# Gated cross-attention: score and weight transposes moved from TensorE to VectorE, softmax on half rows

## The chip, the cores and the metric

The kernel runs on one core of a Trainium2 chip. The metric is the device time of one execution in microseconds. Five engines work side by side, each through its own queue in order: TensorE (PE, with its weight loads PEld), VectorE (DVE), ScalarE (ACT), GpSimd (POOL) and SyncE (SP), which issues most of the DMAs.

## The reference

Input x has 8 batches of 1024 tokens of 1024 features; each batch has a memory of 64 rows of 512 features. All is float32.

```python
memory_proj = einsum('bme,de->bmd', memory, W_mem)
scores = einsum('bnd,bmd->bnm', hidden_states, memory_proj) / sqrt(D)
attn = softmax(scores, axis=-1)
memory_context = einsum('bnm,bmd->bnd', attn, memory_proj)
gate_input = concatenate([hidden_states, memory_context], axis=-1)
gate = sigmoid(einsum('bnf,df->bnd', gate_input, W_gate) + b_gate)
fused = hidden_states + gate * memory_context
return fused * rsqrt(mean(fused ** 2) + 1e-6) * norm_w
```

## The kernel before

A setup of some 78 us loads the weights, projects the memory (`mp`, the keys, and `mg`, which is the memory times the second half of the gate weights) and prepares sums of weights. Then 16 tiles of 512 tokens follow, 53.8 us each.

The product of a tile with the first half of the gate weights is done by two nested layers of a seven-product scheme for 2x2 block matrices. The outer layer has seven products, in the order 1, 6, 7, 5, 4, 2, 3 (`ORDER`); each is made of seven inner products of four matmul records, one per **slot**, so that a tile has 49 slots. `outer_product` writes the inner products to the PSUM banks `af`, `ed` (two sets, used in turn), `b` (`kB`) and `c` (`kC`). Banks b and c exist once: the next writer has to wait until DVE has read them in `u2 = p1 + kB` and `u3 = u2 + kC`. ACT copies `p1` out of `af`, DVE adds `u2`, `u3`, `u4`, POOL adds u3 and u4 into the blocks of the result (`pre`), and DVE then adds `ed` and `af` (`fin_ed`, `fin_af`). POOL also prepares the left sides of the next outer product (`inner_s`, tiles `l`).

In the outer products 4 and 3, `visit` multiplies the transposed attention weights `attnT` with the memory (tiles `pc`) and adds their gate part to `af` and `ed`. Its first two result tiles lie in banks b and c.

The attention itself is small. `scores` computes the scores transposed (memory rows on partitions: 64 rows for each of two halves of the tokens) into two banks, ACT and DVE join them in `sT`. `transpose_scores` turns `sT` by two PE transposes into PSUM (`sc`), `softmax_a` takes the maximum of each row on DVE and runs four exponentials with bias and row sum on ACT, `softmax_b` takes the reciprocal and scales by four ACT operations, and `transpose_attn` turns the result by two PE transposes (`pa`), from where four ACT copies fill `attnT`. `attn_difference` makes the differences of weights that the gate part needs.

What sets the order is written out by hand: `plan` puts each step in a slot with `at(t0 + n, ...)`, or beside a product with `mid`, and every engine gets its instructions in just that program order (`keep_in_program_order`).

Of the kernel before, what the change touches and what calls it, by code (L numbers as in the profile page):

```python
# [8 lines left out]
F32 = mybir.dt.float32  # L9
AF = mybir.ActivationFunctionType  # L10
ALU = mybir.AluOpType
AX = mybir.AxisListType
# [3 lines left out]
P = 128  # L16
# [4 lines left out]
def tile_gated_cross_attention_rmsnorm(  # L21
# [42 lines left out]
    nc = tc.nc  # L64
    B, N, D = x.shape
    M, E = mem.shape[1:]
# [8 lines left out]
    NPAIR = BM // P  # L75
    SCALE = 1.0 / float(D) ** 0.5
    Q4 = D // 4

    const = ctx.enter_context(tc.tile_pool(name="const", bufs=1))
    gpool = ctx.enter_context(tc.tile_pool(name="gpool", bufs=7))  # L80
# [3 lines left out]
    small = ctx.enter_context(tc.tile_pool(name="small", bufs=1))  # L84
    ps = ctx.enter_context(tc.tile_pool(name="ps", bufs=1, space=PSUM))
    ps_ctx = ctx.enter_context(tc.tile_pool(name="ps_ctx", bufs=2, space=PSUM))
    dram = ctx.enter_context(tc.tile_pool(name="dram", bufs=1, space=DRAM))

    pin = tc.keep_in_program_order

    def mm(o, lhsT, rhs, start, stop):
        pin(nc.tensor.matmul(o, lhsT, rhs, start=start, stop=stop, skip_group_check=True))  # L92

    def tt(eng, o, a, b, op):
        pin(eng.tensor_tensor(o, a, b, op))  # L95
# [4 lines left out]
    def t4k(pool, shape, tag, name):  # L100
        return pool.tile(shape, F32, tag=tag, name=name)
# [31 lines left out]
    for k in range(KD):  # L133
        t = t4k(*((gpool, [P, D], "gate") if k < 7 else (apool, [P, D], "s4")), f"w2_{k}")
# [40 lines left out]
    ident = const.tile([P, P], F32, name="ident")  # L175
# [160 lines left out]


    A, S, L2, O = {}, {}, {}, {}
    sTs, attns, attnTs, scs, dens, mps, mgs = {}, {}, {}, {}, {}, {}, {}
    def where(q, t=0):  # L340
        return q // QPB, (q % QPB) * QT + t * P

# [79 lines left out]
        tt(nc.vector, flat, flat, part, ALU.add)  # L422
        sTs[q] = sT

    def transpose_scores(q):
        sc = ps_ctx.tile([P, 4, M], F32, tag="ctx", name=f"sc{q}")
        sT = sTs.pop(q)
        for t in range(2):
            pin(
                nc.tensor.transpose(  # L430
                    sc[:, 2 * t : 2 * t + 2, :].rearrange("p r m -> p (r m)"), sT[:, t, :], ident
                )
            )
        scs[q] = sc

    def softmax_a(q):
        sc = scs.pop(q)
        mx = t4k(small, [P, 4], "mx", f"mx{q}")
        pin(nc.vector.tensor_reduce(mx, sc, AX.X, ALU.max))
        pin(nc.scalar.activation(mx, mx, AF.Copy, scale=-SCALE))  # L440
        e = attns[q] = t4k(small, [P, 4, M], "e", f"e{q}")
        den = dens[q] = t4k(small, [P, 4], "den", f"den{q}")
        for t in range(4):
            pin(
                nc.scalar.activation(
                    e[:, t], sc[:, t], AF.Exp, bias=mx[:, t : t + 1], scale=SCALE, accum_out=den[:, t : t + 1]
                )
            )

    def softmax_b(q):  # L450
        e, den = attns[q], dens.pop(q)
        pin(nc.vector.reciprocal(den, den))
        for t in range(4):
            pin(nc.scalar.activation(e[:, t], e[:, t], AF.Copy, scale=den[:, t : t + 1]))

    def transpose_attn(q):
        attn = attns.pop(q)
        pa = ps_ctx.tile([P, 2, P], F32, tag="ctx", name=f"pa{q}")
        for t in range(2):
            pin(  # L460
                nc.tensor.transpose(  # L461
                    pa[:, t, :],
                    attn[:, 2 * t : 2 * t + 2, :].rearrange("p r m -> p (r m)"),
                    ident,
                )
            )

        at = attnTs[q] = t4k(small, [P, 8, P], "attnT", f"attnT{q}")
        for g in (1, 0):
            for r in range(2):  # L470
                pin(
                    nc.scalar.copy(
                        at[g * M : (g + 1) * M, 2 * r : 2 * r + 2, :], pa[r * M : (r + 1) * M]
                    )
                )

    def attn_difference(q):
        at = attnTs[q]
        tt(nc.vector, at[M:P, 4:6, :], at[M:P, 0:2, :], at[M:P, 2:4, :], ALU.subtract)
        tt(nc.vector, at[M:P, 6:8, :], at[M:P, 2:6:2, :], at[M:P, 3:6:2, :], ALU.subtract)  # L480

    def load_mp(b):
        mps[b] = t4k(small, [P, KD, M], "mpb", f"mpb{b}")
# [132 lines left out]
    def at(slot, fn, *args):  # L616
        due.setdefault(slot, []).append(lambda: fn(*args))
# [202 lines left out]
    def visit(q, o, pcs, af, ed):  # L820

        row, h, g = EXT[o]
        at_, mg = attnTs[q], mgs[q // QPB]
        second = o in SECOND
        for r, k in ((0, af), (1, ed)):
            cols = slice(h * H, (h + 1) * H)
            for t in TOKENS:
                mm(pcs[r][t, :], at_[0:M, 2 * row + r, t], mg[0:M, cols], True, True)
            if second and r == 0:
                for n, left in ((0, g + r), (1, NEG[o])):  # L830
                    part = mg[M:P, h * H + n * C : h * H + (n + 1) * C]
                    for t in TOKENS:
                        mm(k[t, n], at_[M:P, left, t], part, False, True)
# [193 lines left out]
```

## Time and profile before

| what | value |
| --- | --- |
| median of three runs | 953.74 us (953.54 to 953.8) |
| span of the profiled execution | 951.8 us |
| its own time | not listed apart from its span; the median of the runs is 1.9 us above the span |
| mean granted TensorE clock | 0.997 |
| one tile (414.5 to 468.3 us) | PE busy 53.80, DVE 45.96, ACT 21.79, POOL 39.92 us |
| PE transposes of scores and weights | 32 of `sc`, 32 of `pa` |

The span runs from the first instruction to the last. A row of the timeline gives start and duration in us, engine, line, operation, output and inputs by the program's names, shape and count; brackets hold the idle time of the engine ahead of it and what ended it. Instructions of one engine overlap at their ends, so the step from one start to the next is the price of one on a busy engine.

### The profile page before, as it was taken

What the parts mean: (1) busy time and instruction counts of PE and PEld (TensorE: products, weight loads), DVE (VectorE), ACT (ScalarE), POOL (GpSimd) and SP (SyncE); (2) the same over time, 40 slices, a digit from 0 to 9 for tenths busy, and PEclk for the clock granted to TensorE, in tenths of its full rate; (3) what the DMA queues carried; (4) which work ended last, traced back from release to release, by engine and by line L of the source; (5) the groups of instructions that cost most, each with busy time, mean ns of one, the idle gap of its engine ahead of it and who ended that gap; (6) DMA issues with size and microseconds to landing.
All of it is one profiled execution on the core that took longest, in us unless ns stands there. A gap on an engine that the chain in (4) does not pass through costs nothing.

```text
span 951.8 us, 15584 instructions
## 1 busy us (share of the span) xinstructions
PE 939.9 (99%) x5624; PEld 732.1 (77%) x5624; DVE 806.5 (85%) x1258; ACT 361.9 (38%) x782; POOL 711.0 (75%) x780
## 2 busy tenths in 40 slices
PE   9999999999999999999999999999999999999995
PEld 8546778787877778787877778687877778787773
DVE  6988888888888888888888888888888888888887
ACT  3001235162433525153443526253443526243456
POOL 5997877688676777787686867777686767877683
PEclk9999999999999999999999999999999999999998
DMA  9956664482919365481918366391918466390632
GB/s 377 285 144 161 105 122 112 108 181 48 206 46 185 98 130 131 103 185 39 217 45 174 93 141 138 90 199 32 215 53 166 101 133 144 79 210 25 144 142 89
DMA packets 70923, 128.40 MB, mean 135 GB/s; under 512 B 12352, under 2 KB 49216, under 8 KB 70592
## 3 DMA queue, kind: packets, MB, share of 16 engines
q1 hardware_dynamic: 61664, 93.86, 37.5%
q0 software_dynamic: 9184, 33.56, 19.4%
q8 instruction: 45, 0.74, 0.3%
q14 instruction: 30, 0.25, 0.1%
HBM read 87.56 MB, written 41.68 MB: 136 GB/s over the span
## 4 chain that ended last, share of the span: by engine, by line
PE 97%; DVE 2%; ACT 1%; issue 0%; DVEq 0%
PE af L92 31%; PE ed L92 21%; PE pc L92 10%; PE kC L92 10%; PE kB L92 10%; PE pg L92 5%; PE psT_af L92 5%; PE pm L92 3%; DVE gate L95 1%; PE psT_ed L92 0%; PE pz L92 0%; DVE gate L788 0%; PE sc L430 0%; PE pa L461 0%; PE psT_b L92 0%; PE pt L193 0%
## 5 line engine op out<-in xcount | busy, mean ns | idle before, releaser
L95 POOL TENSOR_TENSOR gate<-gate,u 128x512 f32<-128x512 f32 (+1 forms) x224 | 236.9, 1070 | 187.4 <-DVE u L95 151.3
L685 ACT ACTIVATE gate<-gate 128x512 f32<-128x512 f32 x128 | 80.2, 630 | 225.0 <-DVE gate L95 225.0
L352 DVE STREAM_TRANSPOSE a<-xq 128x512 f32<-128x512 f32 x128 | 141.5, 1108 | 3.4 <-issue 3.4
L95 POOL TENSOR_TENSOR l<-a 128x256 f32<-128x256 f32 x128 | 110.9, 866 | 18.6 <-PE af L92 17.5
L714 DVE SCALAR_TENSOR_TENSOR gate<-gate,ss,nw_sb 128x512 f32<-128x512 f32 x120 | 119.4, 995 | 1.1
L92 PE MATMUL pc<-mg,attnT 64*64 64x512 f32 x512 | 116.8, 595 | 0.1
L92 PE MATMUL ed<-it,l 128*128 128x256 f32 x448 | 115.0, 379 | 0.0
L92 PE MATMUL kB<-it,l 128*128 128x256 f32 x448 | 115.0, 379 | 0.0
L95 DVE TENSOR_TENSOR gate<-gate,pc 128x512 f32<-128x512 f32 x128 | 86.1, 682 | 31.7 <-ACT gate L685 31.7
L901 ACT COPY u<-af 128x256 f32<-128x256 f32 x112 | 40.7, 363 | 182.6 <-PE af L92 182.6
L92 PE MATMUL af<-w,a 128*128 128x256 f32 x384 | 98.5, 379 | 0.0
L92 PEld LDWEIGHTS kB<-it,l 128*128 128x128 f32 x448 | 85.1, 190 | 11.6
L95 DVE TENSOR_TENSOR gate<-gate,ed 128x512 f32<-128x512 f32 x112 | 76.1, 679 | 19.1 <-POOL gate L95 17.5
L92 PEld LDWEIGHTS ed<-it,l 128*128 128x128 f32 x448 | 83.9, 190 | 10.7
L95 DVE TENSOR_TENSOR gate<-gate,af 128x512 f32<-128x512 f32 (+1 forms) x128 | 76.7, 609 | 12.8 <-PE af L92 11.2
L92 PEld LDWEIGHTS af<-w,a 128*128 128x128 f32 x384 | 73.0, 190 | 10.3 <-issue 0.5
L95 POOL TENSOR_TENSOR l<-s 128x256 f32<-128x256 f32 x96 | 78.2, 814 | 3.3 <-DVE it L95 3.3
L92 PEld LDWEIGHTS pc<-mg,attnT 64*64 64x64 f32 x512 | 32.9, 132 | 50.1 <-issue 23.5
L92 PE MATMUL af<-mg,attnT 64*64 64x256 f32 (+1 forms) x384 | 67.4, 456 | 0.0
L92 PE MATMUL ed<-it,a 128*128 128x256 f32 x256 | 67.4, 386 | 0.0
L95 DVE TENSOR_TENSOR u<-u,kC 128x256 f32<-128x256 f32 x112 | 45.9, 410 | 23.8 <-PE kC L92 20.3
L92 PE MATMUL af<-t,s 128*128 128x256 f32 x256 | 65.8, 379 | 0.0
(147 smaller groups left out, 2044.6 us busy)
## 6 DMA issues: line engine op xcount, KB each, us to landing
xq<-in_x SPq DMA_DIRECT2D x64, 512.0 KB, 10.3
gate<-in_x POOLq DMA_DIRECT2D x60, 512.0 KB, 8.4
out<-gate SPq DMA_DIRECT2D x60, 512.0 KB, 3.3
w<-in_w_gate_t SPq DMA_DIRECT2D x8, 512.0 KB, 10.2
w<-in_w_gate_t SPq DMA_DIRECT2D x2, 2048.0 KB, 17.2
mg<-mgd SPq DMA_DIRECT2D x16, 256.0 KB, 5.2
wm<-in_w_mem_t SPq DMA_DIRECT2D x4, 512.0 KB, 6.0
mpd<-mpT SPq DMA_DIRECT2D x4, 512.0 KB, 8.6
```

The costliest lines, as they stand in the source:

```text
L92: pin(nc.tensor.matmul(o, lhsT, rhs, start=start, stop=stop, skip_group_check=True))
L95: pin(eng.tensor_tensor(o, a, b, op))
L352: nc.vector.transpose(A[key][:, :, r * P : (r + 1) * P], chunks(xq[q][:, 4 * t : 4 * t + 4, :], KD)[:, half * KH : (half + 1) * KH],)
L685: pin(nc.scalar.activation(g, g, AF.Sigmoid))
L714: nc.vector.scalar_tensor_tensor(g[:, cols], g[:, cols], rstd[:, t % 2 : t % 2 + 1], nw_sb[:, cols], ALU.mult, ALU.mult,)
L901: pin(nc.scalar.copy(p1, af[:, 0]))
```

## The change

The four PE transposes of a tile go. DVE transposes blocks of 32x32 instead, which leaves a row of 64 memory rows split in two halves of 32 that lie on different groups of 32 partitions. Each half gets its maximum (and its sum) by a DVE reduction; four ACT copies of 32x8 elements bring the other half's value beside it; DVE joins the two. The subtraction of the maximum and the division by the sum are POOL operations over the whole tile, and the exponential is one ACT operation. DVE transposes the weights back into the first two of eight `attnT` blocks; two ACT copies of 64 partitions fill the next two. `visit` and `attn_difference` use the blocks in the new places (`upper`). The steps stand in slots 9, 10, 12, 15, 17, 20 and 23 where they stood in 9, 10, 13, 18 and 22.

```diff
-    def transpose_scores(q):
-        sc = ps_ctx.tile([P, 4, M], F32, tag="ctx", name=f"sc{q}")
...
-                nc.tensor.transpose(
-                    sc[:, 2 * t : 2 * t + 2, :].rearrange("p r m -> p (r m)"), sT[:, t, :], ident
+    def turn_scores(q):
+        sc = scs[q] = t4k(small, [P, 2 * P // B32, B32], "sc", f"sc{q}")
+        pin(nc.vector.transpose(sc.rearrange("p n m -> p (n m)"), sT.rearrange("p t c -> p (t c)")))
+        mx = mxs[q] = t4k(small, [P, 2, 8], "mx", f"mx{q}")
+        pin(nc.vector.tensor_reduce(mx[:, 0], sc, AX.X, ALU.max))
+    def other_half(o, i):
+        for g in range(4):
+            pin(nc.scalar.copy(o[g * B32 : (g + 1) * B32], i[(g ^ 1) * B32 : ((g ^ 1) + 1) * B32]))
+    def spread(v):
+        return v.unsqueeze(2).to_broadcast([P, 8, B32])
+    def softmax_a(q):
+        other_half(mx[:, 1], mx[:, 0])
+    def softmax_b(q):
+        tt(nc.vector, mx[:, 0], mx[:, 0], mx[:, 1], ALU.max)
+        tt(nc.gpsimd, sc, sc, spread(mx[:, 0]), ALU.subtract)
+        pin(nc.scalar.activation(sc, sc, AF.Exp, scale=SCALE))
+    def softmax_c(q):
+        pin(nc.vector.tensor_reduce(den[:, 0], scs[q], AX.X, ALU.add))
+        other_half(den[:, 1], den[:, 0])
+    def softmax_d(q):
+        tt(nc.vector, den[:, 0], den[:, 0], den[:, 1], ALU.add)
+        pin(nc.vector.reciprocal(den[:, 0], den[:, 0]))
+        tt(nc.gpsimd, sc, sc, spread(den[:, 0]), ALU.mult)
+    def turn_attn(q):
+            nc.vector.transpose(
+                at[:, 0:2].rearrange("p t c -> p (t c)"), sc.rearrange("p n m -> p (n m)")
...
-        at(t0 + 9, transpose_scores, q)
+        at(t0 + 9, turn_scores, q)
         at(t0 + 10, softmax_a, q)
-        at(t0 + 13, softmax_b, q)
-        at(t0 + 18, transpose_attn, q)
-        at(t0 + 22, attn_difference, q)
+        at(t0 + 12, softmax_b, q)
+        at(t0 + 15, softmax_c, q)
+        at(t0 + 17, softmax_d, q)
+        at(t0 + 20, turn_attn, q)
+        at(t0 + 23, attn_difference, q)
...
-                    mm(whole[t, :], at_[M:P, g + r, t], mg[M:P, cols], second, True)
+                    mm(whole[t, :], at_[M:P, upper(g + r), t], mg[M:P, cols], second, True)
```

On POOL, before, between the outer products 6 and 5 of the seventh tile (in a name such as `u_7_3085` the 7 is the outer product; `l_6_5` is the left side of outer product 5 in that tile):

```order
L95 TENSOR_TENSOR gate_0_3025<-gate_0_3025,u_6_3030 128x256
L95 TENSOR_TENSOR l_6_5_3090<-s_6_2955 128x256
L95 TENSOR_TENSOR l_6_5_3090<-l_6_5_3090,s_6_2955 128x256
L95 TENSOR_TENSOR l_6_5_3090<-s_6_2955 128x256
L95 TENSOR_TENSOR l_6_5_3090<-s_6_2955,l_6_5_3090 128x256
L95 TENSOR_TENSOR gate_3_3103<-gate_1_3017,u_7_3085 128x512
L95 TENSOR_TENSOR gate_2_3120<-gate_0_3025,u_7_3085 128x256
```

The same place now:

```order
L96 TENSOR_TENSOR gate_0_3019<-gate_0_3019,u_6_3024 128x256
L96 TENSOR_TENSOR sc_3039<-sc_3039,mx_3041 128x256
L96 TENSOR_TENSOR l_6_5_3078<-s_6_2949 128x256
L96 TENSOR_TENSOR l_6_5_3078<-l_6_5_3078,s_6_2949 128x256
L96 TENSOR_TENSOR l_6_5_3078<-s_6_2949 128x256
L96 TENSOR_TENSOR l_6_5_3078<-s_6_2949,l_6_5_3078 128x256
L96 TENSOR_TENSOR gate_3_3097<-gate_1_3011,u_7_3073 128x512
L96 TENSOR_TENSOR sc_3039<-sc_3039,den_3081 128x256
L96 TENSOR_TENSOR gate_2_3109<-gate_0_3019,u_7_3073 128x256
```

The subtraction stands ahead of the four `l` and of the `pre` of outer product 7, the multiplication right behind that `pre`.

On DVE, before, from the end of outer product 7 to the first adds of outer product 4 in the same tile:

```order
L95 TENSOR_TENSOR gate_3_3103<-gate_3_3103,ed_7_3084 128x512
L352 STREAM_TRANSPOSE a_7_3125<-xq_2996 128x4x128
L95 TENSOR_TENSOR gate_2_3120<-gate_0_3025,af_7_3083 128x256
L95 TENSOR_TENSOR gate_2_3120<-gate_2_3120,af_7_3083 128x256
L352 STREAM_TRANSPOSE a_7_3125<-xq_2996 128x4x128
L95 TENSOR_TENSOR attnT_3112<-attnT_3112 64x256 x2
L95 TENSOR_TENSOR u_5_3133<-u_5_3133,kB_5_3146 128x256
L352 STREAM_TRANSPOSE a_7_3155<-xq_2996 128x4x128
L95 TENSOR_TENSOR u_5_3133<-u_5_3133,kC_5_3157 128x256
L352 STREAM_TRANSPOSE a_7_3155<-xq_2996 128x4x128
L95 TENSOR_TENSOR u_5_3133<-u_5_3133,ed_5_3132 128x256
L95 TENSOR_TENSOR u_4_3177<-u_4_3177,kB_4_3184 128x256
```

The same place now, up to the point from which the rows are the same again:

```order
L96 TENSOR_TENSOR gate_3_3097<-gate_3_3097,ed_7_3072 128x512
L468 STREAM_TRANSPOSE attnT_3114<-sc_3039 128x256
L353 STREAM_TRANSPOSE a_7_3118<-xq_2990 128x4x128
L96 TENSOR_TENSOR gate_2_3109<-gate_0_3019,af_7_3071 128x256
L96 TENSOR_TENSOR gate_2_3109<-gate_2_3109,af_7_3071 128x256
L353 STREAM_TRANSPOSE a_7_3118<-xq_2990 128x4x128
L96 TENSOR_TENSOR u_5_3126<-u_5_3126,kB_5_3137 128x256
L96 TENSOR_TENSOR attnT_3114<-attnT_3114 64x256 x2
L353 STREAM_TRANSPOSE a_7_3148<-xq_2990 128x4x128
```

The transpose of the weights is put in ahead of four transposes of the next tile's x, and `attn_difference` has changed places with the kB add of outer product 5. Above this place, the transpose of the scores, the two reductions, the two joins and the reciprocal stand among the adds of outer products 6 and 7.

More of the change, by code (lines that the diff above doesn't have):

```diff
@@ L77, in tile_gated_cross_attention_rmsnorm @@
     Q4 = D // 4
+    B32 = 32
     const = ctx.enter_context(tc.tile_pool(name="const", bufs=1))
@@ L423, in add_scores @@
         sTs[q] = sT
-    def transpose_scores(q):
-        sc = ps_ctx.tile([P, 4, M], F32, tag="ctx", name=f"sc{q}")
+    def turn_scores(q):
         sT = sTs.pop(q)
-        for t in range(2):
-            pin(
-                nc.tensor.transpose(
-                    sc[:, 2 * t : 2 * t + 2, :].rearrange("p r m -> p (r m)"), sT[:, t, :], ident
-                )
-            )
[L434 to L475, printed above, removed]
+        sc = scs[q] = t4k(small, [P, 2 * P // B32, B32], "sc", f"sc{q}")
@@ new lines, in softmax_b @@
+    def softmax_b(q):
+        sc, mx = scs[q], mxs.pop(q)
+        tt(nc.vector, mx[:, 0], mx[:, 0], mx[:, 1], ALU.max)
+        tt(nc.gpsimd, sc, sc, spread(mx[:, 0]), ALU.subtract)
+        pin(nc.scalar.activation(sc, sc, AF.Exp, scale=SCALE))
+    def softmax_c(q):
+        den = dens[q] = t4k(small, [P, 2, 8], "den", f"den{q}")
+        pin(nc.vector.tensor_reduce(den[:, 0], scs[q], AX.X, ALU.add))
+        other_half(den[:, 1], den[:, 0])
+    def softmax_d(q):
+        sc, den = scs[q], dens.pop(q)
+        tt(nc.vector, den[:, 0], den[:, 0], den[:, 1], ALU.add)
+        pin(nc.vector.reciprocal(den[:, 0], den[:, 0]))
+        tt(nc.gpsimd, sc, sc, spread(den[:, 0]), ALU.mult)
@@ new lines, in turn_attn, with upper @@
+    def turn_attn(q):
+        sc = scs.pop(q)
+        at = attnTs[q] = t4k(small, [P, 8, P], "attnT", f"attnT{q}")
+        pin(
+            nc.vector.transpose(
+                at[:, 0:2].rearrange("p t c -> p (t c)"), sc.rearrange("p n m -> p (n m)")
+            )
+        )
+        for g in (1, 0):
+            pin(
+                nc.scalar.copy(
+                    at[g * M : (g + 1) * M, 2:4, :], at[(1 - g) * M : (2 - g) * M, 0:2, :]
+                )
+            )
+    def upper(left):
+        return left ^ 2 if left < 4 else left
@@ L477, in attn_difference @@
     def attn_difference(q):
         at = attnTs[q]
-        tt(nc.vector, at[M:P, 4:6, :], at[M:P, 0:2, :], at[M:P, 2:4, :], ALU.subtract)
-        tt(nc.vector, at[M:P, 6:8, :], at[M:P, 2:6:2, :], at[M:P, 3:6:2, :], ALU.subtract)
+        tt(nc.vector, at[M:P, 4:6, :], at[M:P, 2:4, :], at[M:P, 0:2, :], ALU.subtract)
+        tt(nc.vector, at[M:P, 6:8, :], at[M:P, 0:5:4, :], at[M:P, 1:6:4, :], ALU.subtract)
     def load_mp(b):
@@ L832, in visit @@
                     for t in TOKENS:
-                        mm(k[t, n], at_[M:P, left, t], part, False, True)
+                        mm(k[t, n], at_[M:P, upper(left), t], part, False, True)
             else:
```

3 lines of the change are left out of this document (2 added, 1 removed).

## The prediction

> **What bounds it now.** I read the page's busy times first, then its chain of work.
>
> ```profile
> PE 939.9 (99%) x5624; PEld 732.1 (77%) x5624; DVE 806.5 (85%) x1258; ACT 361.9 (38%) x782; POOL 711.0 (75%) x780
> PE 97%; DVE 2%; ACT 1%; issue 0%; DVEq 0%
> ```
>
> PE is never idle for long and holds 97% of the chain that ends last. So PE work that goes is worth its price, as long as nothing keeps PE waiting in its place. Where PE could begin to wait is seen in the timeline of one tile; I took the seventh. The waits view says that the tiles are alike:
>
> ```profile
> DVE gate L95 <- POOL gate L95: 18.3, 17, 1.1
> ```
>
> One wait of DVE for POOL's `pre`, about 1.1 us, comes back in each of the 16 tiles. First PE's own rows, around the transposes and at the first `visit`:
>
> ```profile
> 414.16 0.38 PE L430 MATMUL sc<-ident,sT 128*128 128x128 f32 x2
> 414.38 1.03 PE L92 MATMUL kC<-t,l 128*128 128x256 f32 x4
> ...
> 422.15 0.38 PE L461 MATMUL pa<-ident,e 128*128 128x128 f32 x2
> 422.37 1.03 PE L92 MATMUL ed<-it,l 128*128 128x256 f32 x4
> ...
> 432.74 1.03 PE L92 MATMUL kC<-t,l 128*128 128x256 f32 x4
> 433.69 0.65 PE L92 MATMUL pc<-mg,attnT 64*64 64x512 f32 x2
> ```
>
> The visit begins 0.95 after the kC ahead of it. Its first tile lies in bank b, so it also waits for DVE's `u<-u,kB` of outer product 4. That this can hold PE up is seen once, in the last tile:
>
> ```profile
> 932.74 1.03 PE L92 MATMUL kC<-w,l 128*128 128x256 f32 x4
> 933.91 0.65 PE L92 MATMUL pc<-mg,attnT 64*64 64x512 f32 x2
> ...
> 933.45 0.41 DVE L95 TENSOR_TENSOR u<-u,kB 128x256 f32<-128x256 f32 x1
> ```
>
> There the add ended at 933.86, and the visit began 0.05 later and 1.17 after kC, not 0.95. So: visit = the later of kC + 0.95 and the end of the kB add + 0.05.
>
> **What goes from PE.** Two transposes take 0.22 from start to start (414.16 to 414.38; 422.15 to 422.37). Four are 0.44 a tile, and 16 tiles 7.0 us: 953.74 - 7.0 = 946.7 if PE waits for nothing new. (The span, 951.8, lies 1.9 under the median of the runs; I add differences to the median.) The by-form row has another number:
>
> ```profile
> L430 PE MATMUL sc<-ident,sT 128*128 128x128 f32 x32 | 6.1, 273 | 0.0
> ```
>
> Its 273 ns is the length of one transpose from entry to exit, most of which lies under its neighbours. The Trainium skill, "TensorE: Matmul & The Clock Gate", Part 4: PE-mode transpose, gives about 275 ns for one inside a kernel. By that price 64 of them would be 17.6 us, and the floor 936; the starts in the trace give 0.11 each, and I go by them.
>
> **What is put on the others.** ACT loses nine small operations and four copies a tile and gets eight tiny copies, one exponential and two copies. The nearest row for a tiny copy is
>
> ```profile
> L440 ACT ACTIVATE mx<-mx 128x4 f32<-128x4 f32 x16 | 3.3, 206 | 47.7 <-DVE mx L439 47.7
> ```
>
> so about 0.2 each, and that row's 47.7 us of idle, 3 a tile, stand just where the first four go. POOL gets two operations of 128x256. DVE gets two transposes, a second reduction and two tiny joins. These lie between DVE's last rest (it waits for kC at 415.45) and the kB add before the visit:
>
> ```profile
> 415.45 0.42 DVE L95 TENSOR_TENSOR u<-u,kC 128x256 f32<-128x256 f32 x1 [0.53 <-PE kC L92]
> 415.79 0.75 DVE L714 SCALAR_TENSOR_TENSOR gate<-gate,ss,nw_sb 128x512 f32<-128x512 f32 x1
> 416.45 0.42 DVE L439 TENSOR_REDUCE mx<-sc 128x4 f32<-128x256 f32 x1
> 416.78 1.97 DVE L95 TENSOR_TENSOR s<-a,s 128x1024 f32<-128x1024 f32 x1
> 418.67 0.41 DVE L95 TENSOR_TENSOR u<-u,ed 128x256 f32<-128x256 f32 x1
> ...
> 419.74 0.18 DVE L452 RECIPROCAL den<-den 128x4 f32<-128x4 f32 x1
> ...
> 420.58 0.74 DVE L714 SCALAR_TENSOR_TENSOR gate<-gate,ss,nw_sb 128x512 f32<-128x512 f32 x1
> ...
> 422.17 0.97 DVE L714 SCALAR_TENSOR_TENSOR gate<-gate,ss,nw_sb 128x512 f32<-128x512 f32 x1
> 423.44 0.42 DVE L95 TENSOR_TENSOR u<-u,ed 128x256 f32<-128x256 f32 x1 [0.30 <-PE ed L92]
> 424.99 0.69 DVE L95 TENSOR_TENSOR gate<-gate,ed 128x512 f32<-128x512 f32 x1 [1.13 <-POOL gate L95]
> 425.60 1.10 DVE L352 STREAM_TRANSPOSE a<-xq 128x512 f32<-128x512 f32 x1
> ...
> 430.68 0.38 DVE L95 TENSOR_TENSOR u<-u,kC 128x256 f32<-128x256 f32 x1
> ...
> 432.00 0.38 DVE L95 TENSOR_TENSOR u<-u,ed 128x256 f32<-128x256 f32 x1
> 433.01 0.42 DVE L95 TENSOR_TENSOR u<-u,kB 128x256 f32<-128x256 f32 x1 [0.63 <-PE kB L92]
> ```
>
> From 425.60 to 432.00 DVE does not rest: what comes late at 425.60 is as late at 432.00. Call that delay X. POOL over the same stretch:
>
> ```profile
> 416.00 1.66 POOL L95 TENSOR_TENSOR gate<-gate,u 128x512 f32<-128x512 f32 x1 [0.83 <-issue]
> 419.21 0.73 POOL L95 TENSOR_TENSOR gate<-gate,u 128x256 f32<-128x256 f32 x1 [1.55 <-ACT e L445]
> 419.90 0.73 POOL L95 TENSOR_TENSOR l<-s 128x256 f32<-128x256 f32 x1
> 420.71 1.20 POOL L95 TENSOR_TENSOR l<-l,s 128x256 f32<-128x256 f32 x1
> 421.87 0.72 POOL L95 TENSOR_TENSOR l<-s 128x256 f32<-128x256 f32 x1
> 422.56 1.17 POOL L95 TENSOR_TENSOR l<-s,l 128x256 f32<-128x256 f32 x1
> 423.69 1.27 POOL L95 TENSOR_TENSOR gate<-gate,u 128x512 f32<-128x512 f32 x1
> ```
>
> From 419.21 POOL works without a break, and the `gate<-gate,ed` of DVE at 424.99 waits for its operation of 423.69. (The row of 419.21 names ACT; its input `u` came from the DVE add that ended at 419.08, which fits as well.) So POOL is the path here, and the change puts a subtraction into it.
>
> Step 1, the scores. Nearest to a DVE transpose of 128x256 is the row of 1.10 for twice the size: half of it, 0.55, to all of it, 1.10; I take 0.60, near the half, since a DVE add of half the size (0.42 against 0.69) has a fixed part too. Reduction 0.42. Both begin in the idle 0.53 ahead of 415.45, from 414.9, and DVE comes to the kC add at 415.85, 0.4 late; the reduction that stood at 416.45 (a step of 0.33) is gone behind it. The large sum `s` starts 0.05 late.
>
> Step 2, `s` against POOL. In the first tile this sum ran without POOL beside it:
>
> ```profile
> 104.30 1.23 DVE L95 TENSOR_TENSOR s<-a,s 128x1024 f32<-128x1024 f32 x1
> ```
>
> In the seventh it took 1.97, with POOL's operation at 416.00 running until 417.66 beside it: 0.74 lost. That operation follows the kC add, now 0.4 later, so `s` loses about 0.3 more. The `u<-u,ed` behind it moves from 418.67 to 419.0, and POOL's 419.21 to 419.55.
>
> Step 3, the subtraction. It needs the joined maximum, at 419.9, when POOL comes to it at 420.2. Nearest row: 0.73, a step of 0.69, from that up to the 1.20 of a POOL operation beside a DVE scalar_tensor_tensor. Now two of the four `l` pay 0.45 each for such neighbours (1.20 and 1.17 against 0.73); the neighbours stay two, so I add 0.69 alone, and the 423.69 becomes 424.75.
>
> Step 4, division and return. `gate<-gate,ed` starts at 426.05. POOL's multiplication runs from 425.98 to 426.71 (same price); DVE's transpose of the weights waits for it until 426.78 and takes a step of 0.52, so the x transposes start at 427.3 and not 425.60: **X = 1.7**. The second reduction (0.33), the joins and the reciprocal (0.18 as nearest row, 0.1 to 0.3 each) and the wait for the exponential, which comes behind the subtraction, delay `u<-u,ed` from 423.44 to about 424.3: still ahead of 426.05, so POOL's wait hides them. If POOL were quicker by 1.3 they would be the path.
>
> Step 5, the visit. The `u<-u,ed` of 432.00 plus a step of 0.34 plus X gives 434.04 for the kB add, 434.46 for its end, 434.51 for the visit. PE could begin at 433.69 - 0.44 = 433.25, so it waits 1.26 and stands 0.82 later than now. PE's kC of 432.74, which needs bank c, is also held, for less: its add of 430.68 ends at 432.76, the matmul was due at 432.30, and its 0.95 ends at 433.8, before the visit. Behind the visit DVE and POOL wait for PE again, and the next tile begins as this one did.
>
> The break-even is X = 0.88; under 0.45 the whole gain stays.
>
> **Sum.** 15 tiles at 0.82 are 12.3. In the last tile there are no x transposes of a next tile, and DVE rests 1.01 at this place:
>
> ```profile
> 917.13 0.42 DVE L95 TENSOR_TENSOR u<-u,kB 128x256 f32<-128x256 f32 x1 [1.01 <-PE kB L92]
> ```
>
> so about 0.4 is lost there. 953.74 + 12.7 = 966.4; I say **966**. X is good to some 0.45: 1.2 gives 959, 2.1 gives 973.
>
> **Rivals.**
> - The whole gain, 946.7. DVE's rests in the stretch (0.53, 0.30, 1.13 and 0.63) are 2.6 us, more than the roughly 2 us of steps that it gets. For it speaks that sum. Against it: the 1.13 is a wait for POOL, and grows with the subtraction instead of taking work in. It needs X under 0.45, that is POOL operations of next to nothing or a shorter chain ahead of them. 0.20.
> - Near break-even, X from 0.75 to 1.0, by the same chain with `s` not held longer and a shorter transpose: 952 to 955.5. 0.10.
> - POOL and DVE shut each other out for whole instructions. `s` lost 0.74 of the 0.88 in which POOL's operation ran beside it. If each of the two scalar_tensor_tensor also keeps POOL out for its 0.66 to 0.74 and not for 0.45, X is 2.15 to 2.2 and a tile loses 1.3: 974. 0.08. The Trainium skill, "SBUF — State Buffer", Who interferes with whom, says that between a VectorE operation with two SBUF inputs and a GpSimd read whoever issues first holds the pair for the whole instruction; the row of 422.17 (0.97 against 0.74, with POOL's `l` of 421.87 untouched at 0.72) agrees, the 1.20 of 420.71 only in part.
> - The DVE transposes cost their upper bound, 1.10 each: X = 2.7, 1.8 a tile, 981. 0.04.
>
> The forecast itself, X between 1.0 and 2.1, has 0.58 and a range of 956 to 973.
>
> **How the numbers follow.** A difference of 0.2%, 1.9 us, is about what a measurement can tell from none. Slower takes the forecast, the two dear rivals and a little of the break-even: 0.58 + 0.08 + 0.04 + 0.01 = 0.71. Same has 0.08, faster 0.21. The range runs from the whole gain, 946.5, to 973: outside lie the two dear rivals and the forecast's ends, under 0.2.
>
> **What would show it.** Right: the visit starts more than 0.95 after kC in the inner tiles, and PE's weight load of `pc` waits there for `u<-u,kB` for about 1 us, 15 times; DVE's wait for POOL ahead of `gate<-gate,ed` stays near 1 us, though DVE comes to it later; a new wait of the weights' transpose for POOL. PE busy falls by some 7 us while the span grows. Wrong: visits at kC + 0.95, `u<-u,kB` of outer product 4 waiting for PE as now. The steps apart: DVE transposes of 128x256 far from 0.6, POOL's two operations far from 0.73, or `s` shorter than 1.97. A step that I have not priced (ACT copies across partition groups, 0.2 each in my count) would have to take over 1 us to become the path.

## The result, and the profile after

The changed kernel takes **960.28 us** (median of 4 runs, 959.95 to 960.49), against 953.77 (953.54 to 953.81) for the kernel before, run beside it: a ratio of 1.0067, 95% interval 1.0053 to 1.0081. The forecast was 966, with slower as the likeliest outcome at 0.71; the time lies inside the range (946.5 to 973), with half of the loss that was forecast: 6.5 us, not 12.7.

The page of the changed kernel, busy times and chain of work (its span is 958.5):

```profile
PE 937.2 (98%) x5560; PEld 724.5 (76%) x5560; DVE 853.3 (89%) x1338; ACT 340.3 (36%) x686; POOL 732.0 (76%) x812
PE 67%; DVE 21%; issue 6%; POOL 4%; ACT 1%; DVEq 0%; POOLq 0%
```

TensorE has less to do and VectorE more, and the chain that ends last is no longer PE alone: a fifth of it is now on DVE, two thirds are still PE. One row of PE's waits is new in most tiles (engine and line, what it waited for, us in all, times, longest):

```profile
PE pc L93 <- DVE u L96: 6.9, 15, 0.5
```

Fourteen of these stand at the first `visit` of the second to the fifteenth tile, where a matmul waits for an add of DVE; the fifteenth is at the second visit of the last tile. In the first tile the first visit starts 1.05 after its kC. The timeline of the seventh tile has PE at both visits:

```profile
434.36 1.10 PE L93 MATMUL kC<-t,l 128*128 128x256 f32 x4
435.94 0.65 PE L93 MATMUL pc<-mg,attnT 64*64 64x512 f32 x2 [0.48 <-DVE u L96]
...
450.89 1.03 PE L93 MATMUL kC<-w,l 128*128 128x256 f32 x4
452.05 0.65 PE L93 MATMUL pc<-mg,attnT 64*64 64x512 f32 x2
```

The first visit starts 1.58 and the second 1.16 after the kC ahead of it; both had 0.95 before. I measure a tile by the starts of the kC ahead of the first visit: 432.74 and, one tile later, 486.53 before, 434.36 and 488.56 after, so 53.79 and 54.20. The 0.41 is, within 0.01, 0.63 of waiting at the first visit and 0.21 at the second, less 0.44 of PE work gone. The 13 steps from the second tile to the fifteenth are all like this one (54.15 to 54.24) and make 5.4 of the 6.5 us. The first step is shorter, 53.54, and the last longer, 55.34: in the last tile PE waits at yet another place, where the step from one product to the next is 1.95 and not 0.86:

```profile
919.34 0.36 ACT L908 COPY u<-af 128x256 f32<-128x256 f32 x1
```

```profile
919.84 1.10 PE L93 MATMUL af<-t,l 128*128 128x256 f32 x4 [0.93 <-ACT u L908]
```

ACT's copy of `af` stands there behind its copies of the weights, which start at 918.61, as DVE's transpose of the weights ends.

What the visit waits for is on DVE, in the same tile, from the kB add of outer product 6 to the kB add of outer product 4:

```profile
416.63 0.41 DVE L96 TENSOR_TENSOR u<-u,kB 128x256 f32<-128x256 f32 x1
416.96 0.43 DVE L430 STREAM_TRANSPOSE sc<-sT 128x256 f32<-128x256 f32 x1
...
417.76 0.41 DVE L96 TENSOR_TENSOR u<-u,kC 128x256 f32<-128x256 f32 x1
...
418.75 2.29 DVE L96 TENSOR_TENSOR s<-a,s 128x1024 f32<-128x1024 f32 x1
420.96 0.41 DVE L96 TENSOR_TENSOR u<-u,ed 128x256 f32<-128x256 f32 x1
...
421.89 0.36 DVE L96 TENSOR_TENSOR mx<-mx 128x8 f32<-128x8 f32 x1
...
425.94 0.69 DVE L96 TENSOR_TENSOR den<-den 128x8 f32<-128x8 f32 x1
...
427.87 0.69 DVE L96 TENSOR_TENSOR gate<-gate,ed 128x512 f32<-128x512 f32 x1 [0.71 <-POOL gate L96]
428.48 0.44 DVE L468 STREAM_TRANSPOSE attnT<-sc 128x256 f32<-128x256 f32 x1
428.84 1.07 DVE L353 STREAM_TRANSPOSE a<-xq 128x512 f32<-128x512 f32 x1
...
435.16 0.40 DVE L96 TENSOR_TENSOR u<-u,ed 128x256 f32<-128x256 f32 x1
435.45 0.43 DVE L96 TENSOR_TENSOR u<-u,kB 128x256 f32<-128x256 f32 x1
```

The kB add ends at 435.88, and the visit begins at 435.94. All the way from 427.87 to there DVE has no rest; the 0.71 ahead of it is a wait for POOL. POOL's rows of that stretch:

```profile
421.50 0.73 POOL L96 TENSOR_TENSOR gate<-gate,u 128x256 f32<-128x256 f32 x1 [1.54 <-DVE u L96]
422.33 0.62 POOL L96 TENSOR_TENSOR sc<-sc,mx 128x256 f32<-128x256 f32 x1
...
426.58 1.26 POOL L96 TENSOR_TENSOR gate<-gate,u 128x512 f32<-128x512 f32 x1
427.80 0.61 POOL L96 TENSOR_TENSOR sc<-sc,den 128x256 f32<-128x256 f32 x1
```

The subtraction of the maximum (`sc<-sc,mx`) stands behind the `pre` of 421.50 and ahead of the four `l` and of the `pre` of 426.58, for which DVE's `gate<-gate,ed` waits. The multiplication (`sc<-sc,den`) ends at 428.41, 0.07 before DVE comes to the transpose of the weights.

So the reading is: DVE's row, with what it waits for, needs 54.20 a tile; PE needs less and waits. DVE waits for POOL above all on the way to the first visit. PE stays in this ring only with the matmuls of the visits, for which DVE waits in turn: its `gate<-gate,af` waits 0.62 for PE behind the first visit (437.97) and 0.75 behind the second (453.27). Its rivals are that PE's own stream became dearer, that the two POOL operations slow DVE by shutting it out, and that the visit's place in the program is at fault, so that the wait goes if the visit or a transpose moves.

### The profile page after: what moved, and what is told of

Same layout as the page of the kernel before. It is cut to its first block, busy times and chain, and to the rows that moved or that the text cites. A ratio compares the mean times of both kernels' runs of the same rounds, so it can differ in the third digit from the quotient of the medians.

```text
span 958.5 us, 15427 instructions
## 1 busy us (share of the span) xinstructions
PE 937.2 (98%) x5560; PEld 724.5 (76%) x5560; DVE 853.3 (89%) x1338; ACT 340.3 (36%) x686; POOL 732.0 (76%) x812
## 4 chain that ended last, share of the span: by engine, by line
PE 67%; DVE 21%; issue 6%; POOL 4%; ACT 1%; DVEq 0%; POOLq 0%
PE af L93 18%; PE ed L93 15%; PE pc L93 10%; DVE a L353 6%; DVE u L96 6%; PE pg L93 5%; PE psT_af L93 5%; DVE gate L96 5%; PE kB L93 5%; PE kC L93 5%; PE pm L93 3%; POOL l L96 2%; POOL gate L96 2%; DVE attnT L96 1%; DVE gate L721 1%
## 5 line engine op out<-in xcount | busy, mean ns | idle before, releaser
L96 POOL TENSOR_TENSOR gate<-gate,u 128x512 f32<-128x512 f32 (+1 forms) x224 | 243.9, 1101 | 176.2 <-DVE u L96 173.5
L96 POOL TENSOR_TENSOR l<-a 128x256 f32<-128x256 f32 x128 | 106.8, 834 | 12.7 <-PE af L93 8.6
L96 POOL TENSOR_TENSOR l<-s 128x256 f32<-128x256 f32 x96 | 71.6, 745 | 3.6 <-PE af L93 3.6
L93 PE MATMUL af<-w,l 128*128 128x256 f32 x256 | 66.2, 381 | 0.0
```

## The experiments

Each time stands beside runs of the kernel before on the same chip (medians of 953.85 to 953.92 in the four batches); a ratio is to these.

**1. What the transposes on PE are worth** (e4). The kernel before, with the four PE transposes taken out and nothing put in:

```diff
-        for t in range(2):
-            pin(
-                nc.tensor.transpose(
-                    sc[:, 2 * t : 2 * t + 2, :].rearrange("p r m -> p (r m)"), sT[:, t, :], ident
-                )
-            )
-        scs[q] = sc
+        scs[q] = sTs.pop(q).rearrange("p t (r m) -> p (t r) m", m=M)
...
-        pa = ps_ctx.tile([P, 2, P], F32, tag="ctx", name=f"pa{q}")
...
+        pa = attn.rearrange("p (t r) m -> p t (r m)", r=2)
```

> The kernel before without its 64 PE transposes (the softmax reads the scores as they lie, and the weights are copied as they lie; everything else stays). My theory: PE is the path there, each pair is worth 0.22 us: 953.8 - 7.0 = 946.8. By the length of one transpose, 0.273 us, it would be 936; if PE's time were hidden, 953.8.

Measured 946.9, ratio 0.9924 (0.9904 to 0.9944). The 64 transposes cost 7.0 us, 0.11 each, the step between their starts. The 275 ns that the Trainium skill gives ("TensorE: Matmul & The Clock Gate", Part 4: PE-mode transpose) match the length of such a row, not what it adds to a stream without gaps.

**2. Is PE still the bound?** (e2) The changed kernel with four idle PE transposes a tile, whose results nothing reads, in the two places they had:

```diff
+    def idle_turns(q, sT, name):
+        sd = ps_ctx.tile([P, 2, P], F32, tag="ctx", name=f"{name}{q}")
+        for t in range(2):
+            pin(nc.tensor.transpose(sd[:, t, :], sT[:, t, :], ident))
...
+        at(t0 + 18, lambda q: idle_turns(q, idle.pop(q), "pd"), q)
```

> The changed kernel with four PE transposes a tile added in the old slots, of the tile sT, into the ctx banks; nothing reads them. My theory: PE waits at the visit anyhow, so 0.43 us more of PE work a tile ahead of it is taken in by the wait of 0.62: 960.3, within 1.5. Rival (PE still sets the pace everywhere, and the loss is a slower PE or more matmul time): 960.3 + 7.0 = 967.

Measured 960.33, ratio 1.0065 (1.005 to 1.008): 7.0 us of PE work, and no change. The first visit of the seventh tile now starts 1.13 after kC:

```profile
434.54 1.02 PE L93 MATMUL kC<-t,l 128*128 128x256 f32 x4
435.67 0.65 PE L93 MATMUL pc<-mg,attnT 64*64 64x512 f32 x2
```

What PE has more to do it waits less: the tile is 54.20 with and without these transposes. Ahead of the first visit, where they stand, PE no longer sets the pace; of PE work behind a visit this run says nothing.

**3. Which part of the softmax sets that row** (e3, e9, e10, e7). Four kernels, each with one edit to the changed kernel. First without both POOL operations, so that the weights are neither shifted nor normalised:

```diff
-        tt(nc.gpsimd, sc, sc, spread(mx[:, 0]), ALU.subtract)
...
-        tt(nc.gpsimd, sc, sc, spread(den[:, 0]), ALU.mult)
```

> The changed kernel without the two POOL operations (the subtraction of the maximum and the division by the sum are left out; all of DVE's and ACT's steps stay). My theory (POOL's chain ahead of the add of ed carries the delay): the kB add of outer product 4 comes some 0.8 us earlier, the first visit is back at 0.95 to 1.05 after kC, 947 to 951. Rival (DVE's own added work, 2.9 us a tile, makes the delay, POOL only waits beside it): 958 to 961.

Measured 952.07, ratio 0.9978 (0.9967 to 0.9988), a little outside what was expected. Then each alone, the first or the second line of that diff:

> Leaves out the subtraction of the maximum on POOL; reduction, copies and join of the maximum stay, and so does the multiplication. Theory: the subtraction (0.62) stands ahead of POOL's u gates, and DVE's ed gate waits for these (0.71 at 427.87), so taking it away brings the whole row behind it on DVE forward by 0.58: gap of the first visit from 1.57 to about 1.0, tile 53.65 to 53.75, 952.0 to 953.5, as without both POOL steps (952.07). Rival: both POOL steps weigh alike, half of the 8.2 us each, 956.2.

> Leaves out the multiplication by the reciprocal on POOL; the weights are not normalised, all else stays. Theory: it ends (428.41) just as DVE comes to the weights' transpose behind the ed gate (428.48), so DVE does not wait for it and its row stays where it is: gap 1.5 to 1.6, 959.0 to 960.5. Rival: both POOL steps weigh alike, 956.2.

Without the subtraction 951.63 (ratio 0.9976, 0.9965 to 0.9986), a little under what was expected; without the multiplication 960.66 (1.007, 1.0055 to 1.0085), a little over. Of the two, the subtraction is the whole, 8.7 us (960.28 less 951.63), and the multiplication nothing. DVE's rows without the subtraction:

```profile
417.62 0.41 DVE L96 TENSOR_TENSOR u<-u,ed 128x256 f32<-128x256 f32 x1
...
423.97 0.69 DVE L96 TENSOR_TENSOR gate<-gate,ed 128x512 f32<-128x512 f32 x1 [0.72 <-POOL gate L96]
...
431.57 0.41 DVE L96 TENSOR_TENSOR u<-u,kB 128x256 f32<-128x256 f32 x1
```

From `u<-u,ed` to `gate<-gate,ed` are 6.35 us, where the changed kernel has 6.91 (420.96 to 427.87): 0.56 less. That is the subtraction's step of 0.58 and the 0.14 that POOL waits ahead of it (below), less about 0.15 that the four `l` take longer without it (3.82 for 3.67). A tile is 53.65, 0.55 less. Both operations have the same length and the same engine; they differ in what stands behind them.

The joins of the halves have two small inputs each, 128x8. They take longer than their size says, so here is a kernel in which they are reductions over one input:

```diff
-        tt(nc.vector, mx[:, 0], mx[:, 0], mx[:, 1], ALU.max)
+        pair = mx.rearrange("p t n -> p n t")
+        pin(nc.vector.tensor_reduce(mx[:, 2], pair[:, :, 0:2], AX.X, ALU.max))
...
-        tt(nc.vector, den[:, 0], den[:, 0], den[:, 1], ALU.add)
+        pair = den.rearrange("p t n -> p n t")
+        pin(nc.vector.tensor_reduce(den[:, 2], pair[:, :, 0:2], AX.X, ALU.add))
```

> The changed kernel with its two joins of half values (128x8) made by a reduction over one input tile and not by a tensor_tensor of two. In the changed kernel's trace they take 0.36 and 0.69 us where the first tile, without POOL beside them, has 0.16. Theory of the shared port (an operation with two SBUF inputs waits for POOL's operation that is running): the joins fall to about 0.16 to 0.2 each, DVE comes 0.7 us earlier to the add of ed, and waits longer for POOL there; the time falls by 0 to 3 us, since POOL is the path at that place. Rival (a tiny operation waits for ACT's copies or for DVE's own last result): the joins keep 0.36 and 0.69.

The views of the tiles `mx` and `den`, with shortest, median and longest in ns, first of the changed kernel, then of this one:

```profile
L96 DVE TENSOR_TENSOR mx<-mx x16: 160/363/366, 96.2 to 909.8; 128x8 f32<-128x8 f32 x16
L96 DVE TENSOR_TENSOR den<-den x16: 159/693/697, 99.2 to 913.8; 128x8 f32<-128x8 f32 x16
```

```profile
L449 DVE TENSOR_REDUCE mx<-mx x16: 156/157/163, 96.0 to 907.5; 128x8 f32<-128x16 f32 x16
L461 DVE TENSOR_REDUCE den<-den x16: 161/164/170, 98.6 to 911.4; 128x8 f32<-128x16 f32 x16
```

Measured 958.21, ratio 1.0045 (1.003 to 1.006): 2.1 us of the 6.5 come from joins of 128x8. The shortest of each in the changed kernel, in the first tile, has the 160 ns that all have with one input; it starts within 0.1 of the end of a POOL operation (96.22 and 96.27, 99.16 and 99.25). The others are over two and four times as long. In the seventh tile each starts in the midst of a POOL operation and ends 0.02 after it: 422.25 and 422.23 for the first, 426.63 and 426.61 for the second. Only the first join is on the path, as DVE's and POOL's rows of this kernel show:

```profile
415.68 0.41 DVE L96 TENSOR_TENSOR u<-u,kB 128x256 f32<-128x256 f32 x1
...
426.78 0.69 DVE L96 TENSOR_TENSOR gate<-gate,ed 128x512 f32<-128x512 f32 x1 [1.24 <-POOL gate L96]
```

```profile
420.56 0.73 POOL L96 TENSOR_TENSOR gate<-gate,u 128x256 f32<-128x256 f32 x1 [1.55 <-DVE u L96]
421.24 0.61 POOL L96 TENSOR_TENSOR sc<-sc,mx 128x256 f32<-128x256 f32 x1
```

The subtraction now starts before POOL's row ahead of it has ended (421.29), where in the changed kernel it started 0.10 after that end (422.23) and 0.08 after the end of the join (422.25). `gate<-gate,ed` comes 11.10 behind the kB add, not 11.24: 0.14 a tile. What the second join saves, 0.5, goes into a longer wait for POOL, 1.24 in place of 0.71. The Trainium skill ("SBUF — State Buffer", Who interferes with whom) says that a VectorE instruction with two SBUF inputs contends with a GpSimd instruction that reads SBUF and one with a single input does not; these rows agree.

**4. Without the maximum** (e6, e11). The exponential is taken of the scores as they are, and the reduction, the copies, the join and the subtraction go. The softmax has the same value; it is safe only where the scaled scores cannot overflow the exponential, as with these inputs.

```diff
-        mx = mxs[q] = t4k(small, [P, 2, 8], "mx", f"mx{q}")
-        pin(nc.vector.tensor_reduce(mx[:, 0], sc, AX.X, ALU.max))
...
-        tt(nc.vector, mx[:, 0], mx[:, 0], mx[:, 1], ALU.max)
-        tt(nc.gpsimd, sc, sc, spread(mx[:, 0]), ALU.subtract)
```

> The changed kernel without the maximum: the exponential is taken of the scaled scores directly (the same softmax by arithmetic). That takes away one DVE reduction, one join, four ACT copies and POOL's subtraction. My theory: POOL's chain is 0.6 to 0.9 us shorter, about what the run without both POOL steps gained; first visit at 1.0 to 1.1, the second still near 1.15, 951 to 954. Rival (POOL's multiplication alone holds the transpose of the weights, the subtraction is hidden): 957 to 960.

Measured **947.11**, ratio 0.9927 (0.9911 to 0.9943): faster than both kernels, and better than I expected. Page and visit of this kernel:

```profile
PE 933.1 (99%) x5560; PEld 726.5 (77%) x5560; DVE 834.2 (88%) x1306; ACT 331.1 (35%) x622; POOL 726.0 (77%) x796
PE 97%; DVE 2%; ACT 1%; issue 0%; DVEq 0%
```

```profile
429.78 1.03 PE L93 MATMUL kC<-t,l 128*128 128x256 f32 x4
430.74 0.65 PE L93 MATMUL pc<-mg,attnT 64*64 64x512 f32 x2
```

PE has the chain to itself again, the visit starts 0.96 after kC, and a tile is 53.35: the whole 0.44 is collected. That e6 is 4.5 us faster than e9, which lacks the subtraction too, comes from DVE. The reduction of the maximum is gone there, and from the kB add of outer product 6 to `u<-u,ed` it needs 3.93 (412.00 to 415.93), where e9 and the changed kernel need 4.34 and 4.33. The stretch behind, to `gate<-gate,ed`, is 6.35 as in e9. If PE sets the tile again, PE work must count again, by the edit of e2 made to this kernel:

```diff
+    def idle_turns(q, sT, name):
+        sd = ps_ctx.tile([P, 2, P], F32, tag="ctx", name=f"{name}{q}")
+        for t in range(2):
+            pin(nc.tensor.transpose(sd[:, t, :], sT[:, t, :], ident))
...
+        at(t0 + 18, lambda q: idle_turns(q, idle.pop(q), "pd"), q)
```

> The kernel without the maximum (947.11) with four idle TensorE transposes a tile in the places they had before. Theory: with no wait left on the visits PE bounds the tile again, so its 0.44 a tile come back in full: tile 53.79, 954.1. Rival: DVE and POOL still set the tile, as where the turns were put back into the changed kernel (no change there), 947 to 948.

Measured 953.73, ratio 0.9999 (0.9989 to 1.0008). The same four transposes a tile that cost nothing in e2 cost 6.6 us here. Taken together, e2 and e11 show in which kernel PE's work ahead of the first visit sets the tile.

**5. Moving the visit, or a transpose, instead** (e1, e8, e5). Three attempts to take the wait away by order alone; all three came out slower than the changed kernel and missed what was expected. At each of the two places two visits run one behind the other, the first into the banks b and c, the second (`pcs`) into two banks of its own. e1 changes their order at both places, e8 at the first only:

```diff
-            visit(q, f, fp, faf, fed)
             pcs = [ps_ctx.tile([P, H], F32, tag="ctx", name=f"pc{q}_{o}_{r}") for r in range(2)]
             visit(q, o, pcs, af, ed)
+            visit(q, f, fp, faf, fed)
```

> The changed kernel with the two calls of visit exchanged: the outer product's own visit, whose tiles lie in the two ctx banks that the transposes left free, goes first, the other one, into banks b and c, 1.7 us later. No work is added or taken away. My theory (the first visit waits in bank b for DVE's kB add of outer product 4, which POOL's longer path made late): the visit starts 0.95 us after kC again instead of 1.57, and the second visit of a tile loses its 0.20 too; a tile falls from 54.20 to some 53.4 us, the time to 947 to 950. Rival (DVE, busy 89%, cannot keep up with PE whatever bank is used): the wait turns up at another bank and the time stays at 957 or more.

> The changed kernel with the two visits exchanged in outer product 4 alone, so that the scores of the next tile, which stand behind the visits of outer product 3 and wait for its banks, are not touched. Swapping both put a wait of 1.5 us ahead of those scores. My theory: the first visit at 0.95 to 1.0 after kC, a gain of 0.6 a tile at that place; in the run with both swapped a wait of 0.34 stood at outer product 2 (its af behind ACT's copy and POOL), and what remains of it is lost: 951 to 956. Rival (DVE cannot keep up, the wait only moves on): 959 or more.

Measured 972.46 (ratio 1.0192, 1.0175 to 1.0209) and 962.22 (1.0085, 1.0064 to 1.0107). The first visit is back at 0.99 to 1.03 after kC in both, as expected, but there are new waits elsewhere. Waits of e1:

```profile
PEld psT_af L93 <- DVE gate L96: 13.5, 15, 0.9
PEld af L93 <- POOL l L96: 10.1, 16, 1.2
PEld psT_ed L93 <- DVE gate L96: 8.9, 15, 0.6
```

and of e8:

```profile
DVE gate L96 <- PE af L93: 29.1, 32, 1.9
PEld af L93 <- POOL l L96: 10.2, 16, 1.3
```

In e8 DVE waits for `af` twice a tile, where it does so once in the changed kernel (12.0 us in 16 times). In both PE comes too early to the `l` that POOL makes and, in e1, to the banks of the next tile's scores, which DVE has not read yet; a tile of e1 is 54.82. In e8 the inner tile is 54.05, 0.15 less than in the changed kernel. It loses that, and more, at the ends: the first kC ahead of a visit starts at 110.73 (109.85 there), the first step is 55.32 (53.54), and in the last tile the second visit starts 2.22 after its kC (1.36). So at the first place alone the swap does gain a little in each inner tile; a kernel with the swap in the inner tiles only was not run. In e5 the last transpose of the next tile's x goes from slot 25, ahead of the visit, to slot 34, behind it:

```diff
-            (20, 0, 0), (21, 1, 0), (23, 2, 0), (25, 3, 0), (37, 2, 1), (38, 3, 1), (42, 0, 1)
+            (20, 0, 0), (21, 1, 0), (23, 2, 0), (34, 3, 0), (37, 2, 1), (38, 3, 1), (42, 0, 1)
```

> The changed kernel with one of the four x transposes ahead of the visit moved from slot 25 to slot 34, behind it. Nothing else changes. My theory (DVE's queue ahead of the kB add of outer product 4 sets the visit): DVE reaches that add a step of 1.0 us earlier, the first visit is back at 0.95 after kC, and a tile falls by up to 0.62, to 53.6: 950.5, if DVE's rests of 0.33 and 0.70 behind the visit take the transpose in; if they do not, the second visit waits for it and the time stays near 957 to 960. Rival (the path runs through POOL to the weights, so moving DVE work that needs no POOL changes nothing): 960.

Measured 975.83, ratio 1.0231 (1.0215 to 1.0247). The first visit is at 1.03, and the transpose is now in the way of something else, seen in the rows of ACT and PE:

```profile
455.05 0.63 ACT L692 ACTIVATE gate<-gate 128x512 f32<-128x512 f32 x1 [2.76 <-DVE gate L96]
455.58 0.35 ACT L908 COPY u<-af 128x256 f32<-128x256 f32 x1
```

```profile
456.08 1.10 PE L93 MATMUL af<-w,l 128*128 128x256 f32 x4 [1.34 <-ACT u L908]
```

ACT's sigmoid waits for DVE's `gate<-gate,af`, which stands behind the moved transpose; the copy of `af` stands behind the sigmoid in ACT's order, and PE waits 1.34 for it. There is no room for 1.1 us of DVE there: a tile of e5 is 55.21.

**6. A maximum that costs POOL nothing** (e12). Each of the eight rows that share a pair of partitions may be shifted by the same number, since a row's softmax is free of its shift. So one maximum is taken over all eight, and it fits into the bias of the exponential:

```diff
-        pin(nc.vector.tensor_reduce(mx[:, 0], sc, AX.X, ALU.max))
+        pin(nc.vector.tensor_reduce(mx[:, 0, 0:1], sc.rearrange("p n m -> p (n m)"), AX.X, ALU.max))
...
-        tt(nc.gpsimd, sc, sc, spread(mx[:, 0]), ALU.subtract)
-        pin(nc.scalar.activation(sc, sc, AF.Exp, scale=SCALE))
+        pin(nc.vector.tensor_reduce(mx[:, 2, 0:1], mx[:, 0:2, 0], AX.X, ALU.max))
+        pin(nc.scalar.activation(mx[:, 2, 1:2], mx[:, 2, 0:1], AF.Copy, scale=-SCALE))
+        pin(nc.scalar.activation(sc, sc, AF.Exp, bias=mx[:, 2, 1:2], scale=SCALE))
```

> Keeps a maximum, but one for each pair of partitions (the eight rows whose halves lie there share one shift, which each row's softmax is free of): the subtraction goes from POOL into the bias of Exp, with a copy of 128x1 on ScalarE for its sign, and both joins take one input. Theory: nothing stands on POOL ahead of its u gates, as without the subtraction (951.63), and the joins give up to 2.1 more (958.21 against 960.28): 949.3 to 951.8, between the kernel without a maximum and before. Rival: the scaled copy makes Exp and the copy of af behind it on ScalarE late, DVE's kB add waits for it, and the gain is lost: 954 or more.

Measured 951.83, ratio 0.998 (0.9971 to 0.9989): 2.0 us less than the kernel before, about the least that can be told from none, at the upper edge of what was expected, and not below e9 as the cheap joins had seemed to promise. The exponential cannot overflow here, but a row that lies far below the largest of its eight can lose its weights to underflow. The sum's join takes one input as in e7. ACT's rows, and DVE's:

```profile
419.58 0.20 ACT L449 ACTIVATE mx<-mx 128x1 f32<-128x1 f32 x1 [3.40 <-DVE mx L448]
419.80 1.28 ACT L450 ACT_TABLE_LOAD   x1
421.10 0.51 ACT L450 ACTIVATE sc<-sc,mx 128x256 f32<-128x256 f32 x1
```

```profile
418.48 0.41 DVE L96 TENSOR_TENSOR u<-u,ed 128x256 f32<-128x256 f32 x1
...
421.64 0.42 DVE L454 TENSOR_REDUCE den<-sc 128x8 f32<-128x256 f32 x1 [0.51 <-ACT sc L450]
...
424.80 0.69 DVE L96 TENSOR_TENSOR gate<-gate,ed 128x512 f32<-128x512 f32 x1 [0.55 <-POOL gate L96]
```

In the changed kernel the table load for the exponential (418.71) lies ahead of a wait of 3.00 for the exponential's input. Here it stands behind the copy that waits for the maximum, and DVE's second reduction waits 0.51 for the exponential. The Trainium skill ("ScalarE: Activation LUTs", What ACT_TABLE_LOAD costs) gives about 1283 ns for the load, as here, and some 1380 more for a drain; no such drain stands in these rows, the exponential starts 0.02 after the load's end.

The late exponential does not set the time, though: behind it DVE still waits 0.55 for POOL's `pre` (423.05 to 424.77). From `u<-u,ed` to `gate<-gate,ed` are 6.32, where e9 has 6.35, and ahead of them DVE needs 4.34 from the kB add (414.14), as in e9, since the maximum is still reduced. So e12 has the row of e9, its later part set by POOL. The 2.1 us of the joins were the subtraction's wait for the first join, and without a subtraction there is no such wait to save.

## Why the prediction came out as it did

**The floor (946.7): right.** e4 gives 946.9, e6 947.11.

**The mechanism: right.** PE's gain is eaten by a wait for `u<-u,kB` of outer product 4 in every inner tile. DVE is late there by a row that leads back to POOL's subtraction, and e9 shows it: the subtraction out, the first visit is at 1.03 after kC (431.00 and 432.03 in the seventh tile). The rule that the visit starts 0.05 behind the add holds to 0.01.

**The size of X: too large, 1.7 where 1.12 was measured.** From the start of DVE's kB add of outer product 6, which was the last before the change's first DVE instruction, 416.63 after and, before:

```profile
414.51 0.41 DVE L95 TENSOR_TENSOR u<-u,kB 128x256 f32<-128x256 f32 x1
```

- Step 1. The kC add comes 1.13 behind it, where it came 0.94: late by 0.19, not by 0.4. A DVE transpose of 128x256 takes 0.43, not 0.60, that of the weights a step of 0.36 (428.48 to 428.84), not 0.52: less than half the price of the double size, without the fixed part that I had argued from the adds.
- Step 2. `u<-u,ed` comes 4.33 behind it, 4.16 before: 0.17 late, not 0.33. The large sum did stay longer, 2.29 for 1.97, as foreseen, since POOL's operation beside it moved as well. The row of 104.30, from which the forecast took this, was misread, though: POOL did work beside it, and its `l` of 104.41 took 1.70. There POOL was held and not DVE, so 1.23 is the price of a sum that is not held.
- Step 3. The subtraction takes 0.62 and a step of 0.58 (422.33 to 422.91), not 0.73 and 0.69: an operation with a broadcast operand of 128x8 is cheaper than the row that I took for it. `gate<-gate,ed` is late by 0.76 (11.24 against 10.48), not by 1.06.
- Step 4. The weights' transpose waits for the multiplication for almost nothing and takes its step of 0.36, so the x transposes are late by 1.12 (12.21 against 11.09). I had 0.64 for this step and it was 0.36. That the multiplication, for all its 0.61, costs nothing is e10.
- The joins were priced at 0.1 to 0.3 and took 0.36 and 0.69. That POOL's wait hides the second is right (e7). The first was to be ready before POOL comes to the subtraction; it comes 0.14 after, and these are the 2.1 us of e7.

**Step 5.** With X of 1.12 the prediction's own rule, X less 0.88, gives 0.24 a tile, and the first visit alone lost 0.19 (0.63 less the 0.44). At `u<-u,ed` ahead of the visit the delay is 1.04 (18.53 against 17.49), so the row keeps it nearly whole, as forecast. X is the part that was mis-sized; the prediction had named "1.2 gives 959" as an edge. By the same measure, to the first x transpose, X is 0.57 in e9 and 0.16 in e6: above and below the 0.45 under which the whole gain was to stay.

**"Behind the visit DVE and POOL wait for PE again": wrong.** It is half of what a tile loses (0.21 of 0.41). From the end of the kB add ahead of the first visit to that of the one ahead of the second, DVE needs 16.12 (435.88 to 452.00, by the row below), PE from the first visit to the second only 15.90 (435.94 to 450.89, and 0.95). Before, DVE came to this stretch with a lead and waited for PE at its end; now that the first visit starts at the very end of DVE's add, there is no lead, and PE waits 0.2 again. The add ahead of the second visit, before and after:

```profile
448.89 0.42 DVE L95 TENSOR_TENSOR u<-u,kB 128x256 f32<-128x256 f32 x1 [0.51 <-PE kB L92]
```

```profile
451.62 0.38 DVE L96 TENSOR_TENSOR u<-u,kB 128x256 f32<-128x256 f32 x1
```

In e9 the same stretch is again 16.12 (431.57 and 0.41 to 447.72 and 0.38), the second visit 1.14 after its kC, though the first hardly waits; in e6, where the first visit waits for PE alone, the second is at 0.96. That DVE's row here is the cause is read from these starts; no run shortened it by itself.

**The last tile: wrong.** The forecast put 0.4 there, at the kB add; that visit starts 0.96 after kC, and what is lost, about 1.1, is the wait for ACT's copy of `af` shown above, which the prediction did not have.

**The signs.** The first two came: late first visits in the tiles before the last, and there waits for `u<-u,kB`, of PE's weight load 0.85 to 0.88. DVE's wait for POOL is 0.71, not near 1; the transpose of the weights hardly waits for POOL; and PE busy fell by 2.7 us (939.9 to 937.2), not by some 7. Part of PE's waiting counts as busy in that row: e6, with as many matmuls and no wait at the inner visits, has 933.1.

**The rivals.** The whole gain needed X under 0.45; e6 shows that it is there to be had, in this case without the maximum. POOL and DVE holding each other up does occur in the joins and is worth 2.1 us. The rival that it named, POOL kept out for the whole of each scalar_tensor_tensor, did not come: the two `l` beside these took 1.06 and 1.19 (423.71 and 425.42), about the 1.20 and 1.17 of before.

## What to carry over

Work that is moved off a full engine pays only as far as the engines that take it are late for nothing: follow the row from the first new instruction to the point where the full engine waits next, and look for the new instruction that stands ahead of a wait. Of two operations of the same length on the same engine, one cost 8.7 us and the other nothing. When an engine that was not the bound becomes it, adding idle work to the old bound ahead of the wait (e2, e11) tells so in one run. Moving the wait about (e1, e5, e8) did not shorten this kernel.

## What the runs showed of the hardware that was not expected

- A DVE join of two inputs of 128x8 took 0.16 us in the first tile and, as a median, 0.36 or 0.69, where it started in the midst of a POOL operation; with one input it took 0.16 to 0.17 in all.
- A DVE transpose of 128x256 float32 took 0.43 us, one of 128x512 1.07 to 1.12: more than double for the double size. The two differ in layout too (the larger one reads four blocks of 128), so that size alone is not shown to be the reason.
- ACT copies of 32x8 from one group of 32 partitions to another took 0.195 us each, four of them 0.81.
- An ACT table load of 1.28 us stood right ahead of the function that needs it and behind every earlier ACT instruction: it lay ahead of a longer wait of ACT (changed kernel) or made the exponential late by the order alone, so that DVE waited 0.51 for it (e12). In e12 that wait was taken in by DVE's next one, for POOL.
